# Convolution tables in row halves: Toeplitz blocks of 64 rows and 128 columns for pairs of channels

## The chip, the cores and the metric

The kernel runs on one core of one Trainium2 chip. The metric is the device time of one execution in microseconds. The core has a TensorE (PE, with a queue of its own for weight loads, PEld), a VectorE (DVE), a ScalarE (ACT), a GpSimd (POOL) and a SyncE (SP) that here only issues transfers; all share 16 DMA engines. The on-chip memory SBUF has 128 partitions; PSUM, where PE writes its products, has eight banks.

## What is computed

`x` is 32 sequences of 64 channels and 1024 positions. Four residual layers are added to it one after the other; only the first is touched here:

```python
def _L0_cond_ref(u, log_dt, C, log_A_real, A_imag, D, length):
    K = _get_kernel(log_dt, C, log_A_real, A_imag, Lq)   # one filter of 1024 taps a channel
    n = 2 * Lq
    kf = jnp.fft.rfft(K, n=n)
    uf = jnp.fft.rfft(u, n=n)
    y = jnp.fft.irfft(uf * kf[None], n=n)[..., :Lq]
    y = y + u * D[:, None]
    mask = (jnp.arange(Lq)[None, :] < length[:, None]).astype(u.dtype)
    return y * mask[:, None, :]
...
x = x + _L0_cond_ref(x, ...)                  # causal convolution, a filter for each channel
x = x + _L1_cond_ref(x, itok_B_0_15, w1)      # a 1024 x 1024 weight for each sequence, picked by id
x = x + _L2_cond_ref(x, itok_B_1_14, w2)      # the same with other weights
x = x + _L3_cond_ref(x, ...)                  # gated feed-forward with low-rank additions by id
```

So the first layer is, for each of 64 channels, a causal convolution of 32 sequences with a filter of 1024 taps, and the two after it read one 4 MB weight for each sequence. All data are 4-byte floats.

## The kernel before, in words

**The convolution as products.** For one channel the convolution is a lower triangular Toeplitz matrix (1024 x 1024) times a 1024 x 32 matrix of inputs. It is cut into 8 x 8 blocks of 128 x 128. All blocks on one diagonal are equal, so eight blocks are enough. The filter (with 128 zeros ahead of it) lies as one row of `kp` in DRAM; a transfer whose source steps by one element per partition and by one element along the row reads it as a table `hk` of 128 partitions x 1024, in which partition p holds the filter shifted by p. Columns d x 128 to (d+1) x 128 of that table are the block of diagonal d. The inputs `uf` are laid out on the host (`xf`, L1481) with positions inside a block reversed, so that the shift runs the right way.

**`convolve` (L1372)** handles four channels (HA = 4) and is called 16 times; these calls are called groups here, 0 to 15. It loads `uf` for its four channels (512 KB, two buffers), then, for each of two pairs of channels, a tile `hk` (L1385) that holds two tables, 1024 KB, with three buffers (in group 0 each table is a transfer of its own). For each channel eight matmuls (L1404) with a full 128 x 128 block and N = 256, 224, ... 32 moving columns add up in PSUM: diagonal d multiplies the first 8 - d input blocks. Both channels of a pair write one PSUM bank. After each pair DVE multiplies the bank by the length mask into `tmp` (through the helper `tt`, L1172). After both pairs POOL adds the first quarter of the sequences to `x0`, copies the others to `co`, and stores them to `cd` in DRAM.

**Filters.** `kernels(g)` (L1315) makes the filters of 4 or 8 channels (`GROUPS`), nine times in all: POOL and DVE prepare angles and exponents, ACT takes exponentials and sines, PE multiplies (`pk`, L1346 and L1355), ACT copies the product to `ks` (L1364) and stores it to `kp` (L1366). Kernels 0 and 1 are made ahead; `convolve` calls the others through `between` (`more`), ahead of the matmuls of its second pair. ACT also computes the exponentials of the sizes for later kernels (L1249), in an order set by a scheduler.

**First weights.** While the convolution runs, SP also loads weights for the first adapter pass. `first_weights` (L178) yields one 512 KB load at each step, for "own" tiles (16 early ones, four in a tile of `x` that is not yet used, and 7 late ones that exist once the filters are made and `places` is called) and nine tiles of a rotating pool. `fetch(n)` issues n of them: 8 in group 0, two in each of the next three groups, one in each group after that, and two in each of the last two groups (one with each pair); whatever is left is issued after the convolution.

**The first adapter pass** (`adapter`, L297, its matmuls L304) takes 128 weight tiles for two layers in order, 16 column-tiled matmuls each; the tiles that are not yet on chip rotate through the pool as PE frees them. Everything after that (the other three quarters of the sequences, the feed-forward) follows it.

**Order.** PE's program order is the one written in the code (`manual_schedule`); the other engines' orders are the scheduler's. SP issues its transfers in its program's order: where one has to wait for a free buffer or for a store to `kp`, the later ones wait with it.

Of the kernel before, what the change touches and what calls it, by code (L numbers as in the profile page):

```python
# [9 lines left out]
F32 = mybir.dt.float32  # L10
# [9 lines left out]
P = 128  # L20
B, H, L = 32, 64, 1024
NS = 64
KT = L // P
# [8 lines left out]
MB = 4  # L32
MG = 2
NG = FM // MG
EARLY = 16
LEFT_AT = 11
LATE = 7
FIRST_LOADS = 8
MORE_LOADS = 3
ROTATING = 9  # L40
HA = 4
SEG = 2
# [10 lines left out]
KROW = P + L  # L53
# [23 lines left out]
def kernel(  # L77
# [55 lines left out]
    epool = first.enter_context(tc.tile_pool(name="epool", bufs=1, side="right"))  # L133
    early = [epool.tile([P, L], F32, tag=f"e{i}", name=f"early{i}") for i in range(EARLY)]
    early += [
# [995 lines left out]
def convolution(tc, cst, consts, xt, xf, ssm, lens, x0, cd, ps_tile, fetch, places):  # L1131
# [10 lines left out]
    nc = tc.nc  # L1142
    with ExitStack() as ctx:
# [5 lines left out]
        s3 = ctx.enter_context(tc.tile_pool(name="s3", bufs=3))  # L1149
# [14 lines left out]
        def small():  # L1164
            n_small[0] += 1
            return s1.tile([P, H], F32, tag=f"sm{n_small[0]}", name=f"sm{n_small[0]}")
# [4 lines left out]
        def tt(o, a, b, op):  # L1171
            nc.vector.tensor_tensor(o, a, b, op)  # L1172
            return o
# [80 lines left out]
        x, y = small(), small()  # L1254
# [6 lines left out]
        t, em, ep = small(), small(), small()  # L1261
# [110 lines left out]
        def convolve(kp, row, ha, between):  # L1372


            uf = s3.tile([P, HA, KT, B], F32, tag="uf", name=f"uf{ha}", bufs=2)
            nc.sync.dma_start(uf, xf[:, ha : ha + HA])
            if ha == 0:
                fetch(FIRST_LOADS)
            tmp = g0_2.tile([P, HA, KT * B], F32, tag="tmp", name=f"tmp{ha}")
            for i in range(0, HA, 2):  # L1380
                hk = s3.tile([P, 2, L], F32, tag="hk", name=f"hk{ha + i}")

                for j in range(0, 2, 1 if ha == 0 else 2):
                    n = 1 if ha == 0 else 2
                    nc.sync.dma_start(  # L1385
                        hk[:, j : j + n],
                        bass.AP(
                            tensor=kps.tensor,
                            offset=kp[row + i + j : row + i + j + 1, 1:2].offset,
                            ap=[[1, P], [KROW, n], [1, L]],  # L1390
                        ),
                    )

                first, last = ha <= HA * MORE_LOADS, ha > H - HA * MORE_LOADS
                if ha and i == 0:
                    fetch(1 + first)
                elif ha and last:
                    fetch(1)
                if i:
                    between()  # L1400
                ps = ps_tile(f"pc{ha + i}").rearrange("p (i t) -> p i t", i=2)
                for j in range(2):
                    for d in range(KT):
                        nc.tensor.matmul(  # L1404
                            ps[:, j, d * B :],
                            hk[:, j, d * P : (d + 1) * P],
                            uf[:, i + j, : KT - d, :].rearrange("p k b -> p (k b)"),
                            start=(d == 0),
                            stop=(d == KT - 1),
                        )  # L1410
                tt(
                    tmp[:, i : i + 2, :],
                    ps,
                    maskf.unsqueeze(1).to_broadcast([P, 2, KT * B]),
                    ALU.mult,
                )
            xv = x0.rearrange("p k (b h) -> p k b h", h=H)[:, :, :, ha : ha + HA]
            tv = tmp.rearrange("p i (k b) -> p k b i", b=B)[:, :, :BC, :]
            nc.gpsimd.tensor_tensor(xv, xv, tv, ALU.add)
            co = g0.tile([P, NCK - 1, HA * KT, BC], F32, tag="co", name=f"co{ha}")  # L1420
            tv = tmp.rearrange("p i (k c b) -> p c (i k) b", k=KT, b=BC)[:, 1:]
            nc.gpsimd.tensor_copy(co, tv)
            nc.gpsimd.dma_start(
                cd.rearrange("c p g e -> p c g e")[:, :, ha // HA],
                co.rearrange("p c i b -> p c (i b)"),
            )
# [14 lines left out]
        maskf = mask.rearrange("p k b -> p (k b)")  # L1441
        for g, n in enumerate(GROUPS):
            h0 = sum(GROUPS[:g])

            def more():
                if len(ready) < min(g + 3, len(GROUPS)):
                    ready.append(kernels(len(ready)))
                    if len(ready) == len(GROUPS):
                        making.close()
                        places()  # L1450

            for i in range(0, n, HA):
                convolve(ready[g], i, h0 + i, more)
# [20 lines left out]
def _layouts(np, v):  # L1474
    cont = np.ascontiguousarray

    x = v["x"]

    xt = x.reshape(NCK, TC, KT, P).transpose(3, 0, 2, 1)

    xf = x.reshape(B, H, KT, P)[..., ::-1].transpose(3, 1, 2, 0)  # L1481

    def states(a):
        return np.concatenate([a.T, a.T])
# [58 lines left out]
    for i, (m0, m1) in enumerate(BLOCKS):  # L1543
        n = 2 * (m1 - m0)
        ad[:, i, :, :n] = a[:, :, :, m0:m1].reshape(NE, P, n, R)
    left = left.reshape(P + REST, NE, R).transpose(1, 0, 2)
    n = 2 * BLOCKS[0][1]
# [71 lines left out]
```

## Time and profile before

| what | us |
|---|---|
| median of 3 runs | 2312.29 (2309.24 to 2312.61) |
| the profiled execution's span | 2313.8 |
| PE busy in it | 2249.8 |
| first and last convolution matmul (`pc`, start) | 29.1 and 193.8 |
| convolution matmuls, busy | 153.3 |
| first adapter pass | 195.8 to 329.8 |
| granted TensorE clock, mean | 0.998 |

PE and PEld are the TensorE's matmuls and weight loads; each 4-byte matmul instruction appears as two records in the trace. `pc` is the PSUM tile of the convolution, `pa` that of an adapter, `pk` that of the filters. "L1404" is line 1404 of the kernel. A line of a time view gives busy microseconds and, in brackets, the number of records; a wait is put down to what released it.

### The profile page before, as it was taken

The numbers are of one execution on the slowest core, as the hardware profiler recorded it, in microseconds if no ns is written. First come the engines' busy times: TensorE is split into PE (matmuls) and PEld (weight loads), VectorE is DVE, ScalarE is ACT, GpSimd is POOL, SyncE is SP. The second block draws the span as 40 slices with busy tenths as digits, with TensorE's granted clock in tenths as the row PEclk, the third lists the DMA queues.
The fourth block names the chain that finished last, engine by engine and source line by source line (L and its number), as shares of the span: only waits on it lengthen the run. The fifth ranks groups of instructions, "written<-read, shape, count | busy, mean of one in ns | idle before, by whom it ended". The sixth has DMA issues, their size and how long they took to land.

```text
span 2313.8 us, 53743 instructions
## 1 busy us (share of the span) xinstructions
PE 2249.8 (97%) x21706; PEld 1868.0 (81%) x21706; DVE 1320.6 (57%) x2791; ACT 380.0 (16%) x822; POOL 270.6 (12%) x388
## 2 busy tenths in 40 slices
PE   5999989999999999999999999999999999999999
PEld 4996557787777789688778889688769889799998
DVE  7511127567446776546535676646535676477585
ACT  4300001011001112111102212121102212121220
POOL 3423003111101121000000011000000011100000
PEclk9999999999999999999999999999999999999999
DMA  8999997879997957879997957879997947285582
GB/s 306 354 370 394 407 403 280 317 289 354 365 343 293 350 174 258 304 285 360 350 357 279 358 167 265 297 292 358 355 351 288 363 152 276 87 298 203 191 280 68
DMA packets 201802, 684.96 MB, mean 296 GB/s; under 512 B 26178, under 2 KB 28482, under 8 KB 201042
## 3 DMA queue, kind: packets, MB, share of 16 engines
q1 hardware_dynamic: 169714, 590.77, 69.5%
q0 software_dynamic: 25184, 82.37, 9.6%
q10 hardware_dynamic: 6656, 8.39, 1.0%
q8 instruction: 171, 2.80, 0.5%
q14 instruction: 77, 0.63, 0.1%
HBM read 614.02 MB, written 67.40 MB: 295 GB/s over the span
## 4 chain that ended last, share of the span: by engine, by line
PE 78%; DMA 14%; issue 5%; DVE 2%; POOL 1%; POOLq 0%; SPq 0%; ACT 0%; DVEq 0%
PE pq L664 28%; PE po L1063 22%; PE pa L304 11%; DMA wa<-in_w 7%; PE pc L1404 5%; PE pf L573 5%; PE pr L797 3%; DMA wa<-sums 2%; DMA sums<-kept 1%; PE pe L456 1%; DMA hk<-kp 1%; PE pl_d L427 1%; DMA kp<-ks 1%; DMA wf<-in_wg 0%; DMA wr<-in_wr 0%
## 5 line engine op out<-in xcount | busy, mean ns | idle before, releaser
L304 PE MATMUL pa<-wa,x 128*32 128x256 f32 x7760 | 449.1, 381 | 19.3 <-DMA wa<-in_w 16.8
L664 PE MATMUL pq<-xd,wa 128*128 128x128 f32 x3360 | 415.9, 275 | 1.3 <-DMA wa<-sums 0.9
L304 PEld LDWEIGHTS pa<-wa,x 128*32 128x32 f32 x7760 | 241.8, 110 | 209.9 <-DMA wa<-in_w 49.1
L664 PEld LDWEIGHTS pq<-xd,wa 128*128 128x128 f32 x3360 | 395.0, 192 | 2.3 <-DMA wa<-sums 2.2
L664 PE MATMUL pq<-xd,wb 128*128 128x128 f32 x2520 | 324.1, 276 | 0.6 <-DVE x L316 0.4
L664 PEld LDWEIGHTS pq<-xd,wb 128*128 128x128 f32 x2520 | 300.7, 192 | 4.7 <-DVE x L316 0.6
L314 DVE STREAM_TRANSPOSE y<-pa 128x512 f32<-128x512 f32 x64 | 45.9, 717 | 286.6 <-PE pa L304 286.6
L1063 PE MATMUL po<-act,wd 128*128 128x256 f32 x640 | 168.6, 386 | 0.0
L1404 PE MATMUL pc<-uf,hk 128*128 128x256 f32 (+7 forms) x1024 | 153.3, 312 | 12.2 <-DMA hk<-kp 9.5
L1063 PE MATMUL po<-actd,s 128*128 128x256 f32 x640 | 164.2, 379 | 0.0
L1063 PE MATMUL po<-actd,wd 128*128 128x256 f32 x640 | 164.2, 379 | 0.0
L1404 PEld LDWEIGHTS pc<-uf,hk 128*128 128x128 f32 x1024 | 148.4, 195 | 16.6 <-issue 7.9
L355 POOL DMA_INDIRECT bgu<-in_bgu,rows x44 | 51.4, 1168 | 924.0 <-PE pe L456 827.2
L573 PE MATMUL pf<-xd,wf 128*128 128x256 f32 x640 | 150.9, 381 | 0.0
L1063 PEld LDWEIGHTS po<-act,wd 128*128 128x128 f32 x640 | 117.8, 190 | 29.9 <-issue 14.6
L482 DVE TENSOR_TENSOR s<-wd 128x256 f32<-128x256 f32 x80 | 33.8, 423 | 184.1 <-PE po L1063 184.0
L573 PEld LDWEIGHTS pf<-xd,wf 128*128 128x128 f32 x640 | 121.2, 191 | 17.4
L1063 PEld LDWEIGHTS po<-actd,s 128*128 128x128 f32 x640 | 121.6, 190 | 16.5
L1063 PEld LDWEIGHTS po<-actd,wd 128*128 128x128 f32 x640 | 121.6, 190 | 16.5
L1095 ACT COPY uo<-po 128x256 f32<-128x256 f32 x48 | 17.9, 373 | 622.3 <-PE po L1063 620.2
L573 PE MATMUL pf<-xd,s 128*128 128x256 f32 x480 | 115.9, 385 | 3.9 <-DVE up L607 2.7
L573 PEld LDWEIGHTS pf<-xd,s 128*128 128x128 f32 x480 | 91.0, 191 | 20.0 <-DVE up L607 4.4
(235 smaller groups left out, 2566.4 us busy)
## 6 DMA issues: line engine op xcount, KB each, us to landing
wa<-in_w SPq DMA_DIRECT2D x485, 512.0 KB, 7.0
wa<-sums SPq DMA_DIRECT2D x210, 512.0 KB, 5.8
wb<-parts SPq DMA_DIRECT2D x120, 384.0 KB, 5.3
wd<-in_wd SPq DMA_DIRECT2D x80, 512.0 KB, 7.0
wb<-in_wq SPq DMA_DIRECT2D x90, 384.0 KB, 5.9
hk<-kp SPq DMA_DIRECT2D x30, 1024.0 KB, 8.8
sums<-kept POOLq DMA_DIRECT2D x30, 1024.0 KB, 7.2
wf<-in_wg SPq DMA_DIRECT2D x20, 512.0 KB, 7.1
```

Of the source, the lines that this page charges most:

```text
L304: nc.tensor.matmul(acc[i * S : (i + 1) * S, s * 256 : (s + 1) * 256], xs[c][:, kt, lo + s * S : lo + (s + 1) * S], wt[:, i * 256 : (i + 1) ...
L314: nc.vector.transpose(y, acc)
L355: nc.gpsimd.indirect_dma_start(out=t, out_offset=None, in_=table, in_offset=bass.IndirectOffsetOnAxis(ap=at_, axis=0),)
L427: nc.tensor.matmul(ps[pair(j)], at[:, i, pair(j)], x_i[:, 2 * H * j : 2 * H * (j + 1)], start=(i == 0), stop=(i == n - 1),)
L456: nc.tensor.matmul(ps[:, at_ * 2 * H : (at_ + 1) * 2 * H], bt[pair(j), g], tms[table][pair(j)], start=(g == 0), stop=True, skip_group_chec ...
L482: nc.vector.tensor_add(s1, a21, a22)
L573: nc.tensor.matmul(ps, ws[j][:, kt, :], xb[j][:, kt, :], start=start and kt == 0, stop=kt == KH - 1, skip_group_check=True,)
L664: nc.tensor.matmul(ps[:, to * TQ : (to + 1) * TQ], w[i][:, k, :], xb[:, j, SLOT[i], k, :], start=start and k == 0 and to == 0, stop=k == K ...
L797: nc.tensor.matmul(ps, wts[i][:, kt, :], xs[c][:, kt, :], start=(kt == 0), stop=(kt == KT - 1),)
L1063: nc.tensor.matmul(pss[j], *term, start=(s0 == m0 and i == 0 and home[j] % 2 == 0), stop=(end and i == len(terms) - 1 and not late), skip_ ...
L1095: nc.scalar.copy(u1, p1)
L1404: nc.tensor.matmul(ps[:, j, d * B :], hk[:, j, d * P : (d + 1) * P], uf[:, i + j, : KT - d, :].rearrange("p k b -> p (k b)"), start=(d == ...
```

## The change

One row block of the Toeplitz matrix is now 64 rows high and 128 columns wide. A pair of channels shares one table tile: channel 0 of the pair lies on partitions 0 to 63, channel 1 on partitions 64 to 127, each with 64 + 1024 columns. Each half is loaded by a transfer of its own (64 x 1088, 278.5 KB), and there are four buffers of the tile. Inputs are laid out the same way: partitions 0 to 63 hold channel 0 of the pair, 64 to 127 channel 1, and positions are split into 64-row blocks of even and odd number; the bytes of `uf` are the same. A pair takes 16 steps of 64 rows, and each step is two matmuls, one on each row half, that write to two different PSUM banks. A bank now holds one channel of each of the group's two pairs, so both evictions come after the second pair.

There are two more early tiles (18), and `fetch` is called otherwise: 8 in group 0 and two in every group after it, until none is left.

```diff
-EARLY = 16
+EARLY = 18
 LEFT_AT = 11
 LATE = 7
 FIRST_LOADS = 8
-MORE_LOADS = 3
+PAIR = 2
+HP = P // PAIR
...
-            uf = s3.tile([P, HA, KT, B], F32, tag="uf", name=f"uf{ha}", bufs=2)
-            nc.sync.dma_start(uf, xf[:, ha : ha + HA])
+            uf = s3.tile([P, HA // PAIR, 2, KT * B], F32, tag="uf", name=f"uf{ha}", bufs=2)
+            nc.sync.dma_start(uf, xf[:, ha // PAIR : (ha + HA) // PAIR])
             if ha == 0:
                 fetch(FIRST_LOADS)
             tmp = g0_2.tile([P, HA, KT * B], F32, tag="tmp", name=f"tmp{ha}")
-            for i in range(0, HA, 2):
-                hk = s3.tile([P, 2, L], F32, tag="hk", name=f"hk{ha + i}")
-
-                for j in range(0, 2, 1 if ha == 0 else 2):
-                    n = 1 if ha == 0 else 2
+            halves = [slice(r * HP, (r + 1) * HP) for r in range(PAIR)]
+            banks = [ps_tile(f"pc{ha}_{r}").rearrange("p (i t) -> p i t", i=HA // PAIR) for r in range(PAIR)]
+            for i in range(HA // PAIR):
+                hk = s3.tile([P, HP + L], F32, tag="hk", name=f"hk{ha}_{i}", bufs=4)
+                for r in range(PAIR):
+                    h = row + PAIR * i + r
                     nc.sync.dma_start(
-                        hk[:, j : j + n],
+                        hk[halves[r]],
                         bass.AP(
                             tensor=kps.tensor,
-                            offset=kp[row + i + j : row + i + j + 1, 1:2].offset,
-                            ap=[[1, P], [KROW, n], [1, L]],
+                            offset=kp[h : h + 1, 1:2].offset,
+                            ap=[[1, HP], [1, HP + L]],
                         ),
                     )
-
-                first, last = ha <= HA * MORE_LOADS, ha > H - HA * MORE_LOADS
                 if ha and i == 0:
-                    fetch(1 + first)
-                elif ha and last:
-                    fetch(1)
+                    fetch(2)
                 if i:
                     between()
-                ps = ps_tile(f"pc{ha + i}").rearrange("p (i t) -> p i t", i=2)
-                for j in range(2):
-                    for d in range(KT):
+                for e in range(-1, PAIR * KT - 1):
+                    k0 = (e + 1) // 2
+                    for r in range(PAIR):
                         nc.tensor.matmul(
-                            ps[:, j, d * B :],
-                            hk[:, j, d * P : (d + 1) * P],
-                            uf[:, i + j, : KT - d, :].rearrange("p k b -> p (k b)"),
-                            start=(d == 0),
-                            stop=(d == KT - 1),
+                            banks[r][:, i, k0 * B :],
+                            hk[halves[r], (e + 1) * HP : (e + 1) * HP + P],
+                            uf[halves[r], i, e % 2, : (KT - k0) * B],
+                            start=(e < 0),
+                            stop=(e == PAIR * KT - 2),
+                            skip_group_check=True,
                         )
+            for r in range(PAIR):
                 tt(
-                    tmp[:, i : i + 2, :],
-                    ps,
-                    maskf.unsqueeze(1).to_broadcast([P, 2, KT * B]),
+                    tmp.rearrange("p (i r) t -> p r i t", r=PAIR)[:, r],
+                    banks[r],
+                    maskf.unsqueeze(1).to_broadcast([P, HA // PAIR, KT * B]),
                     ALU.mult,
                 )
...
-    xf = x.reshape(B, H, KT, P)[..., ::-1].transpose(3, 1, 2, 0)
+    xf = x.reshape(B, H // PAIR, PAIR, KT, 2, HP)[..., ::-1]
+    xf = xf.transpose(2, 5, 1, 4, 3, 0).reshape(P, H // PAIR, 2, KT * B)
```

## The prediction

> **What bounds the kernel now.** I read the time slices first, then the chain that ended last, then busy time by stage, the waits and the transfers. The slices say that the PE is saturated nearly everywhere except at the start; in the first four slices (0 to 231 us) the DMA engines are as busy as the PE.
>
> ```profile
> PE   5999989999999999999999999999999999999999
> ...
> DMA  8999997879997957879997957879997947285582
> ```
>
> The last work to end is PE work in the feed-forward part, which this change does not touch; the convolution is 5% of that chain through its matmuls and 1% through its tables. So the change can only move the moment at which everything after the convolution starts, and what is left to load then. Cut out of the chain, the convolution (times are start and length in us) reads:
>
> ```profile
> 37.07 7.53 DMA kp<-ks
> ...
> 46.21 11.11 DMA hk<-kp
> ...
> 61.17 9.05 DMA hk<-kp
> ...
> 82.04 18.52 PE pc L1404 x128
> ...
> 101.22 18.52 PE pc L1404 x128
> ```
>
> 128 matmul records are two groups of four channels, so a group costs the PE 9.26 us and a pair of channels 4.63; where the chain shows `hk<-kp`, the PE waits for a table. Counted from the end in records, the runs at 82.04 and 101.22 hold groups 5 to 8: group 7 ends at 101.22 + 9.26 = 110.5. Group 1 starts at 41.2 (pairs 1 and 2 run as one from 36.57 for 9.38 us). Groups 1 to 7 thus took 69.3 us for 64.8 of matmuls; groups 8 to 15 took 83.6 (the last matmul ends at 194.1) for 74.1.
>
> Busy time by stage (window; length; PE, PEld, DVE, ACT, POOL; clock, DMA share, GB/s):
>
> ```profile
> 60.00:90.00 30.00, 26.45 (x184) 25.66 (x184) 21.21 (x38) 18.30 (x26) 14.69 (x17) 0.94 0.95 337
> 90.00:120.00 30.00, 30.00 (x232) 29.28 (x231) 7.18 (x13) 1.44 (x4) 9.68 (x12) 1.00 0.98 374
> ...
> 150.00:195.00 45.00, 41.49 (x291) 39.77 (x289) 6.23 (x9) 0.00 (x0) 9.74 (x13) 1.00 1.00 391
> ...
> 195.00:330.00 135.00, 123.52 (x2058) 68.14 (x2059) 22.08 (x37) 4.08 (x4) 16.68 (x29) 1.00 1.02 401
> ```
>
> PE and DMA are both full here. A group moves 2.10 MB of tables, 0.52 of `uf`, about 0.52 of one first weight and 0.39 of `cd`: 3.54 MB in 9.26 us, 382 GB/s, which is the measured rate. The last row is the first adapter pass: it runs at the DMA's pace.
>
> **The change part by part.**
>
> *Matmuls.* 16 steps of two 64-row halves replace 2 x 8 full-array instructions; the records double to 2048, and the lengths N are the same list twice per step. If the two halves run side by side, a pair still costs 4.63 us. The nearest row is the row-tiled gather product: 32 records of 128 columns, four row tiles to four banks, in 1.39 us.
>
> ```profile
> 337.36 1.39 PE L456 MATMUL pe<-tm_g,bgu 32*128 32x128 f32 x32
> ```
>
> One every 36 ns or so, where the pc records come every 144.7 ns (18.52/128): row tiles do overlap. I cost this at 0; if they did not, it costs 148 us (a rival below).
>
> *Bytes.* 34 table loads of 33.6 MB in all become 64 loads of 64 x 1088 x 4 = 278.5 KB, 17.8 MB. A group now needs 1.114 MB of tables, 0.92 MB of `uf` and `cd`, and its first weights at 0.524 MB.
>
> *Rate.* Here the change can turn on itself: every table load lands on 64 partitions, and no load of the stage before does. The nearest rows are 64-partition loads later in the kernel:
>
> ```profile
> 1335.50:1337.50 2.00, 2.00 (x16) 1.92 (x16) 1.58 (x7) 0.27 (x1) 0.83 (x1) 1.00 0.90 209
> 1337.50:1344.00 6.50, 6.50 (x69) 5.58 (x71) 6.28 (x13) 1.04 (x1) 0.00 (x0) 1.00 1.03 255
> 1345.00:1347.00 2.00, 2.00 (x11) 1.77 (x10) 1.93 (x7) 0.29 (x1) 0.00 (x0) 1.00 1.01 397
> ```
>
> The first is one 64-partition load from SP: 209 GB/s with the engines 90% busy. The second mixes two such loads by gather (0.51 MB) with 1.13 MB on 128 partitions; at the third row's 397 GB/s those take 2.85 us and leave 3.65 us for 0.51 MB, 140 GB/s. [...] I take the row, 209; the ends are 140 and the full 385.
>
> *Groups 1 to 7.* The order of SP's instructions after the change issues 23 first weights among these (31 in all before `uf` of group 7, less 8 at the start), where before it was about one each. Full-width `uf` + `cd`: 0.917 MB at 385 GB/s = 2.4 us a group. A weight: 1.36 us. Tables at 209: 5.33 us. DMA time: 7 x (2.4 + 5.33) + 23 x 1.36 = 85.4 us, against the 69.3 these groups took: **+16.1**. At 140 the tables take 7.96 and the sum is 103.8, +34.5; at 385, 2.9 and 68.4, -0.9. Group 0 has the same DMA time as before (8 weights; 2.23 MB at 209 is 10.7 us, 4.2 MB at 385 is 10.9), so group 1 starts as before.
>
> *Table stores.* The changed order on ACT puts kernel 2's copy and store behind the exponential of kernel 4's sizes, and kernel 3's behind that of kernel 6. Before, these exponentials ran at 43.23 and 64.72 and the stores were issued at 37.07 and 52.80. So the stores move to at most about 44 and 62, and kernel 2's lands some 6 us later. SP waits for it in order, with `uf`, later tables and weights behind:
>
> ```profile
> SPq L1385 <- DMA kp<-ks: 11.6, 2, 8.7
> ```
>
> SP idle is DMA idle in a stage that now lacks DMA time. Bounds 0 (the queue is deep enough) and +8 (all 6 us and part of the second); I take **+4**; at the full rate 2.
>
> *Groups 8 to 15.* Only 7 weights fall here. DMA: 8 x 7.73 + 7 x 1.36 = 71.4 us; PE: 74.1 + 1.3 for the last two kernels' matmuls (0.66 each) = 75.4, against 83.6. At most -8.2; with 4 us of slack some of the table waits stay, so **-5** (at 140: 92.4 us of DMA, +9; at full rate -7).
>
> *First adapter pass.* Two more first weights, and the eight late ones that still landed until about 200, 6 us after the last pc, have landed before. Before: 6.1 us of pending loads + 92 tiles x 1.31 us (0.524 MB at 401 GB/s) = 126.6 from the convolution's end. After: 90 tiles = 117.9, and SP has nothing to load until the first rotating tile comes free, about 0.7 + 2.9 us after the end: 121.5. **-5.** With the PE as cover: it was busy 123.5 of these 135 us, so no more than this comes off.
>
> *Evictions.* As many of the same size (0.70 us), but both at a group's end: at the convolution's end two stand before POOL's add, **+0.7**. Inside, PE needs a bank again only several groups later. SP's 30 extra table issues at about 0.5 us are 15 us in 165, in which SP waits for PE anyhow: 0.
>
> *Sum.* 16.1 + 4 - 5 - 5 + 0.7 = +10.8 on the profiled 2313.8 us (its span, which the runs' 2312.29 median lies 1.5 below): 2324.6, so **2323** as a median.
>
> **The rivals.** A measurement of this kernel tells about 0.2% (4.6 us) from no change.
>
> 1. *Half-width loads at the full rate, or near it; faster.* A mix with full-width loads could fill what half-width ones leave idle. Then -0.9 + 2 - 7 - 5 + 0.7 = -10: 2302. For it: half the table bytes, and the middle window's 255 GB/s for a mix. Against it: 209 with little else in flight. It decides above about 330 GB/s (groups 1 to 7: 71 us).
> 2. *Balance.* At 285 GB/s the tables take 3.91 us a group, groups 1 to 7 need 75.5 us (+6.2), and 6.2 + 3.5 - 5.5 - 5 + 0.7 is nil: 2312. It holds between 245 and 330.
> 3. *Mixed loads at the gathers' 140 GB/s; much slower.* 34.5 + 9 + 4 - 5 + 0.7 = +43: 2355. For it: this is the only window with half and full widths mixed. Against it: gathers by POOL are another kind of transfer.
> 4. *The row halves don't run at once.* 32 pairs x 4.63 = +148, less the DMA terms that it would hide: about 2445. The row-tiled product speaks against it.
>
> **How the numbers follow.** Tables at 160 to 245 GB/s, my forecast: 0.50, own range 2317 to 2340. Gather-like, below 160: 0.17. Balance: 0.14. Faster: 0.16. Serial halves: 0.03. So slower 0.70, same 0.14, faster 0.16. The range runs from rival 1's value to just past rival 3's, 2302 to 2356; it leaves out about half of each, and rival 4.
>
> **What would show it.** In the changed profile: pc at about 18.5 us per 256 records where nothing waits; between 41 and 111 us the DMA share near 1 but GB/s well under 385 (23 weights, 7.8 MB of tables, 6.4 of the rest: 26 MB in 85 us, near 310); PE waits on `hk<-kp` there, not late; group 7 ending near 130; kernel 2's store at 43 to 44. The first pa would start at 195.8 + 16 = 212 and the pass take about 5 us less. The forecast is wrong if that stage moves more than 340 GB/s, if the first pa starts before 200, or if table loads take no longer per byte than weights.

## The result

The changed kernel takes 2341.8 us (four runs, 2336.7 to 2349.2) where the kernel before takes 2312.0: the ratio is 1.0137, with a 95% interval of 1.0112 to 1.0162, so it is slower by about 30 us. The forecast was 2323 in a range of 2302 to 2356, with 7 chances in 10 for slower. Direction and range held; the size was a third of what was measured.

The time slices of the profile after, over 2335.1 us (that execution took 2336.7):

```profile
span 2335.1 us, 55827 instructions
...
PE   5699989999999999999999999999999999999999
...
DMA  7987998889997965879998966889997957376582
```

In the second slice (58 to 117 us) PE has fallen from 9 tenths to 6. The DMA engines are at 8 and 7 tenths in the third and fourth slices (117 to 234 us), where they stood at 9: PE and the DMA engines both have idle time in the convolution now, at different moments. Two windows of the same profile say where (window; length; PE, PEld, DVE, ACT, POOL busy; clock, DMA share, GB/s). They are cut at the group borders that the matmul records show, groups 1 to 7 (pairs 2 to 15) and groups 8 to 15 (pairs 16 to 31):

```profile
42.70:141.00 98.30, 76.82 (x972) 75.53 (x972) 37.33 (x75) 26.64 (x40) 29.98 (x37) 0.86 0.93 263
141.00:223.50 82.50, 78.67 (x1068) 77.63 (x1070) 10.39 (x17) 0.72 (x2) 19.16 (x24) 0.96 0.74 221
```

The same groups of the kernel before:

```profile
41.20:115.00 73.80, 69.56 (x523) 67.59 (x522) 43.14 (x74) 28.27 (x41) 32.05 (x37) 0.98 0.94 341
115.00:194.10 79.10, 75.95 (x554) 73.82 (x557) 11.07 (x16) 0.72 (x2) 19.27 (x24) 1.00 1.00 382
```

The forecast ends group 7 of the kernel before at 110.5 us. In the matmul records pair 15, its last, runs from 110.4 to 115.1, so the forecast's two bases, 69.3 and 83.6 us, hold 13 and 17 pairs instead of 14 and 16.

Groups 1 to 7 take 98.3 us instead of 73.8 (+24.5). Groups 8 to 15 take 82.5 instead of 79.1 (+3.4), though the DMA engines are busy for only 0.74 of that time. So transfers crowd in the first half of the stage and are missing in the second. The convolution ends at 223.5 instead of 194.1 (+29.4), and the feed-forward's first work (`pl_g`, right after the adapter pass) starts at 359.6 instead of 331.7 (+27.9). What comes after that was 6.7 us shorter in this execution (1975.4 against 1982.1), but it lies between 1973.5 and 1987.5 in the profiles of the experiments below, so one execution of each kernel doesn't show a gain there.

The matmuls themselves are as fast as before. Where nothing waits, a pair of channels takes 4.77 us from its first record to its last, before and after, though the records have doubled (the kernel before, then the changed one; behind the second bar stands PE's idle time ahead of these matmuls):

```profile
L1404 PE MATMUL pc<-uf,hk 128*128 128x256 f32 (+7 forms) x1024 | 153.3, 312 | 12.2 <-DMA hk<-kp 9.5
L1402 PE MATMUL pc<-uf,hk 64*128 64x64 f32 (+7 forms) x2048 | 165.0, 320 | 29.8 <-issue 15.4
```

The 165.0 us of busy time against 153.3 come from first pairs after a wait, which run at a lower granted clock (0.63 to 0.74 on average over the five pairs of the table below). Pair 6, for one, starts at 69.59 us after a wait of 6.0, and the clock around its start is half of the full one:

```profile
66.10:72.90 6.80, 3.31 (x16) 3.34 (x18) 5.75 (x12) 4.54 (x9) 0.54 (x2) 0.50 0.57 162
```

Of the idle time, 29.8 us against 12.2, the very first pair has 4.4 (before: 4.8). Nearly all the rest falls on five pairs:

| pair (group) | PE idle before it, us | the pair itself, us |
|---|---|---|
| 6 (3) | 6.0 | 6.5 |
| 8 (4) | 6.0 | 6.5 |
| 10 (5) | 3.4 | 7.4 |
| 12 (6) | 5.7 | 7.1 |
| 24 (12) | 3.8 | 7.6 |
| any other from 13 to 23 | 0 to 0.6 | 4.8 |

In SP's order four or five first weights stand behind the inputs and tables of each of the groups 2 to 5, and so ahead of those of groups 3 to 6. Four of the seven late ones stand ahead of the inputs of group 12.

What SP waited for most between 40 and 142 us (line, what ended the wait, us in total, times, longest):

```profile
SPq L1387 <- DMA kp<-ks: 22.2, 2, 12.3
SPq L1387 <- DMA early<-in_w: 11.2, 8, 2.1
```

The first is the wait for the late stores to `kp` that the forecast names. The second is a table load that waits for the landing of a first weight, with which it shares no data: in this trace the transfers of SP and the stores of ACT share eight completion semaphores, and none of the 66 between 40 and 142 us starts before the transfer ahead of it on its semaphore has landed. The table load at 82.27 us, for one, has the semaphore of the first weight issued at 74.56, eight places ahead of it, which landed at 82.26.

### The profile page after: what moved, and what is told of

It reads as the page before. It is cut to its first block, busy times and chain, and to the rows that moved or that the text cites. A ratio compares the mean times of both kernels' runs of the same rounds, so it can differ in the third digit from the quotient of the medians.

```text
span 2335.1 us, 55827 instructions
## 1 busy us (share of the span) xinstructions
PE 2256.5 (97%) x22730; PEld 1881.4 (81%) x22730; DVE 1314.7 (56%) x2791; ACT 379.6 (16%) x822; POOL 269.8 (12%) x388
## 4 chain that ended last, share of the span: by engine, by line
PE 79%; DMA 8%; issue 2%; DVE 1%; POOL 0%; POOLq 0%; SPq 0%; DVEq 0%
PE pq L665 28%; PE po L1064 23%; PE pa L305 13%; PE pf L574 8%; DMA wa<-in_w 7%; PE pr L798 3%; PE pe L457 2%; PE pl_d L428 1%; DMA sums<-kept 1%; DMA wr<-in_wr 0%; PE pl_g L428 0%; PE pl_u L428 0%; PE po L1072 0%; PE pe_rest L457 0%; POOLq L390 0%
## 5 line engine op out<-in xcount | busy, mean ns | idle before, releaser
L1402 PE MATMUL pc<-uf,hk 64*128 64x64 f32 (+7 forms) x2048 | 165.0, 320 | 29.8 <-issue 15.4
L1402 PEld LDWEIGHTS pc<-uf,hk 64*128 64x128 f32 x2048 | 161.2, 198 | 32.9 <-issue 19.7
```

The costliest lines, as they stand in the source:

```text
L1402: nc.tensor.matmul(banks[r][:, i, k0 * B :], hk[halves[r], (e + 1) * HP : (e + 1) * HP + P], uf[halves[r], i, e % 2, : (KT - k0) * B], sta ...
```

## The experiments

Three theories were to be told apart. A, the forecast's: table loads on 64 partitions are slow. B: the place of the first weights in SP's queue. C: the late table stores. D, the fall of the clock after each wait, was added on seeing the profile. All ratios are to the kernel before on the same chip.

### e1 and e3: one load over 128 partitions

```diff
-                for r in range(PAIR):
-                    h = row + PAIR * i + r
-                    nc.sync.dma_start(
-                        hk[halves[r]],
-                        bass.AP(
-                            ...
-                            ap=[[1, HP], [1, HP + L]],
+                h = row + PAIR * i
+                load = nc.sync.dma_start(
+                    hk,
+                    bass.AP(
+                        ...
+                        ap=[[KROW, PAIR], [1, HP], [1, HP + L]],
```

In e1 the weights are tied (with an order of issue, not a wait) about where the changed kernel has them; in e3 they are spread evenly as in e2.

> The changed kernel with one edit of substance: both halves of a table tile come by one load over all 128 partitions (32 loads instead of 64, the same bytes), and the first weights stand in nearly the same places of SP's order (23 of them among groups 1 to 5 or 7). Theory A, the forecast's: table loads on 64 partitions at about 209 GB/s are what makes groups 1 to 7 wait. Then table bytes now move at about 385 GB/s, the DMA time of these groups falls by 7 x 2.4 = 17 us, and the time from 2342 to about 2324 (2318 to 2328). Theory B, the place of the weights in the queue: tables stand behind four or five weights a group whatever their own rate, the stalls of five pairs stay, and the time stays at 2335 to 2342.

> Both edits at once: one 128-partition load for a table tile, and two weights a group. DMA time of a group 2.4 + 2.9 + 2.7 = 8.0 us, below PE's 9.3. Theories A and B: PE bounds the convolution except where a table store is late; its end at about 188 to 193 instead of 194 before the change, and the adapter pass 2 to 5 us shorter; time 2300 to 2309, faster than before the change. Theory C: the stalls around the stores of the third and fourth filters stay at 10 us or more, time 2315 or more.

Measured: 2587.4 us (1.1185, 1.1161 to 1.1209) and 2588.5 us (1.1190, 1.1166 to 1.1215). No theory had expected a loss of 275 us, and as a test of the width both failed. A stretch of e1 in which little but table loads is under way (the second line is the rate in 40 slices of 440 to 453 us):

```profile
DMA  9985211111111111011110111111111111111111
GB/s 356 367 216 153 78 27 54 54 54 54 54 54 54 54 54 54 40 54 54 54 54 40 54 54 54 54 53 52 52 52 53 54 54 54 54 54 54 54 52 52
```

The load moves 54 GB/s at a tenth of the 16 engines' time, as if two of them did the work: 2/16 of the 401 GB/s that the adapter pass moved is 50, as an estimate, and 54 were measured. The source pattern of this load begins with the pair, 2; that of the kernel before, whose window in e6 moved 390 GB/s, begins with the 128 partitions. Whether this is the reason was not tried. So the half bytes at full rate, the premise of the forecast's first rival, stayed untested.

### e2: two weights a group

```diff
-                if ha and i == 0:
-                    fetch(2)
+                if ha:
+                    with tc.issue_after(load.ins):
+                        fetch(1)
```

(`load` is the second half's table load of each pair.) The changed kernel asks for two weights a group too, but nothing ties them to it: the scheduler puts 3, 5, 4, 5, 5, 1, 0, 0, 0, 0, 4, 3, 0, 0 between the `uf` loads of groups 1 to 15. With the tie it is 3 and then 2 throughout.

> The changed kernel with its 64-partition loads, but the first weights are tied behind the table loads of their own group, one behind each pair's, so that two a group are issued through all groups instead of three to five in groups 1 to 6, none in 7 to 10 and seven in 11 and 12. Theory A: the DMA time of a group is 2.4 + 5.3 + 2 x 1.36 = 10.4 us against 9.3 to 9.6 of PE, so the convolution ends at about 43 + 15 x 10.4 = 199 instead of 223, time about 2318 (2312 to 2324). Theory B: with no crowd ahead of the tables PE is the bound but for the waits for table stores; convolution's end about 193 to 196, time 2305 to 2311. Theory C, the late table stores on ACT alone: 2335 to 2342.

Measured: 2330.2 us, 1.0067 (1.0044 to 1.0089). The order alone gives back 12 of the 30 us, with the stores as late as in the changed kernel (43.60 and 62.20 us); theory C is out as the whole cause, B in its pure form missed by 19 or more, and A, with 2324 as its upper end, by 6. The convolution ends at 214.6. From 82 to 200 us:

```profile
82.00:200.00 118.00, 108.00 (x1408) 106.52 (x1406) 19.55 (x31) 4.78 (x9) 28.19 (x34) 0.94 1.03 278
```

Now the DMA engines are full all through this window, and PE still waits 2 to 3 us in every second group or so. Groups 8 to 15 take 95.1 us with the wait ahead of them, 11.9 each, where the sum of rates gave 10.4. With 3.08 MB a group that is 259 GB/s: two weights a group are more than a stage with half-width tables can carry at PE's pace, and even the even order leaves 17 us of the loss.

### e4: the stores early

```diff
-            with behind(*((stored, 1 if g > 1 else -1) if g < 4 else (turned, g - 1))):
+            with behind(*((stored, 1 if g > 1 else -1) if g < 4 else (turned, g - 1))), behind(stored, g // 2 if g in (4, 6) else -1):
                 done = nc.scalar.activation(rho, rho, AF.Exp)
```

> The changed kernel with one edit: ACT takes the third and fourth filters' copies and stores ahead of the exponentials behind which they had come to stand, as before the change. Theory C: SP's waits for stores (35 us in the changed kernel, 12.3 at the longest, with the DMA engines idle for some 10 of them) fall, and with them the time by 8 to 12 us, to about 2332. The forecast's own term was 4 us: about 2338. Theories A and B allow less than 5.

Measured: 2343.3 us (2332.1 to 2348.7), 1.0122 (1.0082 to 1.0163): no change against the changed kernel's 1.0137. The edit did less than it was meant to. The stores of kernels 2 and 3 went out at 41.47 and 60.07 us instead of 43.74 and 62.35, not at the 37.07 and 52.80 of the kernel before, because ACT still takes the next kernel's sines ahead of them. SP's waits for stores over the first 330 us of e4:

```profile
SPq L1387 <- DMA kp<-ks: 27.5, 3, 10.4
SPq L171 <- DMA kp<-ks: 12.1, 2, 7.8
```

They sum to 39.6 us; in the changed kernel they were 35.2 (30.9 and 4.3). So 2.3 us less delay is worth nothing that e4's runs, 17 us apart, can show, and on the whole delay e4 doesn't decide; e9 and e10 do, below.

### e5 and e6: the kernel before, with half-width loads, and the control

```diff
-                for j in range(0, 2, 1 if ha == 0 else 2):
-                    n = 1 if ha == 0 else 2
+                for j in range(2):
+                    lo = j * (P // 2)
                     nc.sync.dma_start(
-                        hk[:, j : j + n],
+                        hk[lo : lo + P // 2],
                         bass.AP(
                             tensor=kps.tensor,
-                            offset=kp[row + i + j : row + i + j + 1, 1:2].offset,
-                            ap=[[1, P], [KROW, n], [1, L]],
+                            offset=kp[row + i : row + i + 1, 1 + lo : 2 + lo].offset,
+                            ap=[[1, P // 2], [KROW, 2], [1, L]],
```

e6 keeps the original lines with `range(2)` and `n = 1` in all groups: as many loads of as many bytes, over 128 partitions.

> The kernel before, whose table tiles of 128 partitions and 1024 KB now come by two loads of 64 partitions and 512 KB each; all else, the order on SP too, as before. Theory A (a load on 64 partitions moves at about 205 GB/s): a group's DMA time goes from 9.2 to 2.10 MB/205 + 1.44 MB/385 = 13.9 us, 15 groups take 66 us longer less the first ones' slack, time about 2375 (2360 to 2395). If only the number of loads mattered, it would be as e6.

> The control: the kernel before, whose table tiles come by two loads of 128 partitions and 512 KB each, one for each channel (as it has them in its first group already). The number of loads and the bytes of each are those of e5. Theory A: nothing but SP's 30 more issues, time 2310 to 2316. If the number of loads is what costs (more waits for a free slot among the loads under way), 2330 or more.

Measured: e5 2387.2 us, 1.0316 (1.0296 to 1.0337), +74 us. e6 2316.1 us, 1.0010 (1.0002 to 1.0019), 2.8 us more, at the edge of what was expected. The same window of both, e5 first:

```profile
110.00:190.00 80.00, 64.97 (x428) 62.26 (x428) 8.31 (x13) 1.09 (x3) 11.91 (x15) 0.90 1.03 258
```

```profile
110.00:190.00 80.00, 79.55 (x580) 77.61 (x579) 11.38 (x17) 0.72 (x2) 21.50 (x27) 1.00 1.01 390
```

Both keep the DMA engines busy all the time, for 258 and for 390 GB/s. From the start of pair 15 to that of pair 27 of e5 are 86.6 us, 14.4 a group; less 3.7 us for the 1.44 MB at full width, 10.7 us remain for 2.10 MB: 196 GB/s, if the full-width loads beside them keep their 385. That is near the forecast's 209, and the loss is the width's, not the number of loads'. (In e5's trace the stores of kernels 2 and 3 went out late too, at 43.70 and 61.47 us; pairs 15 to 27 lie behind that.)

### e7: filler for the clock

```diff
+                if i == 0 and ha // HA in FILL:
+                    for _ in range(5):
+                        nc.tensor.matmul(banks[0][:, 0, :246], cst[:, :P], cst[:, :246], start=True, stop=True, skip_group_check=True)
                 for e in range(-1, PAIR * KT - 1):
```

> e2 (two weights a group) with five 128 x 128 matmuls of 246 columns on a constant ahead of groups 2, 4, 8, 10, 12 and 13, in which e2's PE waits 1.9 to 2.9 us for a table and then takes 6.3 to 6.7 us for the first pair instead of 4.8; 2 us of filler each, whose results are overwritten. Theory D (the fall of the clock after a wait is a cost of its own): the six first pairs take 4.8 again, 6 x 1.7 = 10 us less, about 2320. Theory A (the DMA engines bound these groups, so a faster PE only waits longer): no change, 2327 to 2333, with the pairs at 4.8 and longer waits ahead of later pairs.

Measured: 2330.1 us, 1.0073 (1.0057 to 1.0090), the same as e2's 2330.2; the convolution ends at 214.8 (e2: 214.6). The granted clock of the run rose from 0.996 to 0.998, and the filled first pairs took 4.8 to 4.9 us again, but other pairs waited instead (pair 6 for 2.9 us, pair 18 for 2.0, where e2 had 0.1 and none), and the convolution did not end earlier. The slow first pairs were a symptom: with the DMA engines setting the pace, the faster PE waited longer.

### e8: the two halves on two queues

```diff
-                    load = nc.sync.dma_start(
+                    load = (nc.scalar if r and ha >= 16 else nc.sync).dma_start(
                         hk[halves[r]],
```

> e2 with the second half of each table tile loaded by ACT's queue instead of SP's from group 4 on, so that loads of the lower and the upper 64 partitions are under way at once. [...]

Measured: 2334.0 us, 1.0096 (1.0064 to 1.0129), not better than e2. From 100 to 200 us, e8 and then e2:

```profile
100.00:200.00 100.00, 90.90 (x1224) 89.69 (x1223) 13.23 (x22) 1.08 (x3) 22.70 (x28) 0.97 1.03 275
```

```profile
100.00:200.00 100.00, 90.00 (x1149) 88.92 (x1148) 12.42 (x20) 1.09 (x3) 22.22 (x27) 0.93 1.03 273
```

275 against 273 GB/s, where full-width loads moved 390 in e6: from two queues at once the halves gained nothing that shows.

### e9 and e10: each part of the change alone

e9 has the change's tables, loads and matmuls, 16 early tiles and the weights about where the kernel before has them. e10 has the kernel before with its weights where the changed kernel has them, two fewer among groups 1 to 7, as it has two early tiles fewer. Both tie them to the table loads of a group:

```diff
+PACE = {...}   # e9: 2 in groups 1 to 3, 1 in 4 to 13, 2 in 14, the last ones in 15
+               # e10: 3, 5, 4, 5, 4 in groups 1 to 5, 4 in 11, 3 in 12
...
+                if ha:
+                    with tc.issue_after(load.ins):
+                        fetch(PACE...)
```

> The change's tables, loads and matmuls alone: 16 early tiles again and the first weights where the kernel before has them in SP's order (8, then 2 or 3 a group at first, one a group after that, nine in the last group). By the forecast's terms a group takes 2.4 + 1.114 MB/209 + 1.36 = 9.1 us of DMA, as before (half the bytes at half the rate), so no loss is left: 2310 to 2316. If a mix of half-width and full-width loads moves at the 260 GB/s that e2 showed, it takes 2.56 MB/260 = 9.8 us, 0.5 us above PE's pace over 15 groups: 2317 to 2322. If the half width costs more still than that: above 2324.

> The other part alone: the kernel before, its tables, loads and matmuls, with its first weights moved to where the changed kernel has them in SP's order (21 in groups 1 to 5, none in 6 to 10, seven in 11 and 12). Full-width tables take 2.10 MB/385 = 5.45 us a group, just what the forecast gave the half-width ones, so the crowd should cost as much: groups 1 to 7 take 7 x (2.4 + 5.45) + 21 x 1.36 = 83.5 us of DMA against 69.3: 2320 to 2330. If the crowd hurts only with half-width loads: 2310 to 2316.

Measured: e9 2314.8 us, 1.0008 (0.9990 to 1.0027). e10 2338.2 us, 1.0101 (1.0080 to 1.0122). This is the main result. The new layout alone, with its slow half-width loads, costs nothing that can be measured (by the interval at most 0.27%, 6 us). The weights' order alone, with full-width loads and no other change, costs 24 of the 30 us, more than the 2320 to 2330 that were expected. The other 6 us appear only with both together. Groups 1 to 7 and groups 8 to 15 of e10:

```profile
42.35:131.33 88.98, 72.90 (x523) 70.07 (x522) 44.48 (x77) 27.10 (x39) 31.67 (x37) 0.92 0.94 348
131.33:218.00 86.67, 77.72 (x554) 75.39 (x557) 11.06 (x16) 0.72 (x2) 19.07 (x24) 0.96 0.84 297
```

The same of e9:

```profile
42.66:119.50 76.84, 70.90 (x972) 69.64 (x971) 40.11 (x75) 26.36 (x39) 28.33 (x35) 0.96 0.93 247
119.50:195.93 76.43, 75.72 (x1064) 74.32 (x1068) 9.90 (x17) 0.72 (x2) 19.68 (x24) 1.00 1.00 290
```

e10 shows the pattern of the changed kernel: DMA busy and PE waiting first, DMA idle afterwards, the end of the convolution at 218.0. In its groups 1 to 7 the DMA engines were busy for 0.94 of 89.0 us, 83.6 us, as the expected sum of 83.5 had it; what that sum left out are 5.3 us of idle DMA engines there and 7.6 us more in groups 8 to 15. In e9 groups 1 to 7 take 3.0 us longer than in the kernel before and groups 8 to 15, at PE's pace, 2.7 us less. Its adapter pass takes 3.5 us longer, for a reason that was not looked for, and the feed-forward starts 5.4 us later in this execution; what follows was 6.3 us shorter, within the spread named above.

e2 and e9 have the same tables and nearly as many weights, 38 and 36. Up to 178 us e2 has issued 35 of them and e9 27; e9 issues its last nine behind the last table of the convolution, as the kernel before does with eight. e2 takes 17 us more than the kernel before, e9 none. So an even spread is not the best place either.

The two also decide on theory C. In the trace e10 issues the stores of kernels 2 and 3 at 38.23 and 52.76 us, as the kernel before does, and loses 24 us; e9 issues them at 43.41 and 62.00, nearly as late as the changed kernel, and loses nothing in all.

### e11 and e12: the stores on another queue

```diff
-            done = nc.scalar.dma_start(
+            done = nc.gpsimd.dma_start(
                 kp[:, P:].rearrange("h (a b) -> a h b", b=LQ), ks[:, :n]
```

> e2 (the changed kernel with two weights a group) with the filters' stores issued by POOL instead of ACT, so that they take no slot among the eight that the loads of SP and the stores of ACT share. In e2 SP waited 40 us in all for stores. If these waits are what keeps e2 above the kernel before, 5 to 12 us come off: 2318 to 2325. If the DMA engines are full anyhow: 2327 to 2333.

> The kernel before with the same edit, as a candidate that could beat both: SP waited 28 us for stores in it, PE 8 us for tables in the convolution. If the waits for slots cause the stalls at pairs 5 and 7, 3 to 5 us come off: 2307 to 2310. If the convolution's end hangs on the DMA engines' 370 to 390 GB/s alone: 2311 to 2314.

Measured: e11 2341.9 us, 1.0115 (1.0094 to 1.0136), 11 us worse than e2 by the ratios. e12 2316.6 us, 1.0006 (0.9993 to 1.0020), no difference. Neither expectation of e11 held: SP still waited 38.5 us for stores (e2: 39.7), and kernel 2's was issued at 46.6, later than on ACT. Whether that is all of the 11 us was not tried. No version here beats the kernel before.

## Why the prediction was right or wrong

**Right: slower, by the DMA engines, in groups 1 to 7.** 24.5 of the 29.4 us by which the convolution ends later arise there. The step that names 23 first weights among these groups as what overfills the queue is what e10 shows alone.

**Right: the matmuls at nothing.** 4.77 us a pair before and after. The serial-halves rival is out.

**Right: the rate of a half-width load.** 196 GB/s in e5 for the 209 taken. The rivals that hang on the rate being 330 or more, 245 to 330, or 140, are out for this transfer.

**Luck: the range.** The forecast's own case had 2317 to 2340 and just missed 2341.8. The range holds because its upper end stands for tables at 140 GB/s, which e5 rules out.

**Wrong in emphasis: "here the change can turn on itself".** The forecast's own sums said otherwise. Half the bytes at half the rate are the same DMA time: 1.114 MB at 209 is 5.33 us, 2.10 MB at 385 is 5.45. The width cancels what the halving saves, and e9 shows just that. What is left over is the number of weights per group and where they stand. The forecast had both in one sum and gave the blame to the rate.

**Misread: the border between groups 7 and 8.** The runs of matmuls at 82.04 and 101.22 begin with the second pair of a group, behind a kernel's `pk` matmuls; the forecast took them to begin with the first. That made its base for groups 1 to 7 short by 4.5 us and the other one long by 4.5. Its +16.1 is +11.6 on the right base, its -5 is -0.5, and at most -3.7 could come off groups 8 to 15, not -8.2. The two errors cancel in its sum.

**Mis-sized: groups 1 to 7, 85.4 us of DMA time and 4 for the stores.** That is +15.6 on the right base; measured +24.5. The window has 98.3 us at a DMA share of 0.93, which is 91.4 us busy and 6.9 idle. So 2.9 us of the miss are idle DMA engines and 6.0 are transfers that took longer than their own rates add up to. (From 41 to 111 us, where the forecast looked for near 310 GB/s, 265 moved at a DMA share of 0.90.) The same shows between 90 and 120 us, with the DMA engines never idle:

```profile
90.00:120.00 30.00, 20.95 (x262) 20.64 (x261) 3.15 (x7) 3.08 (x5) 4.01 (x5) 0.84 1.03 299
```

These 30 us moved 9.0 MB, of which 2.05 MB were tables by the size of their packets; at 209 and 385 GB/s that is 9.8 + 18.0 = 27.8 us (28.5 with e5's 196). Where half-width and full-width loads mix, the sum of their rates was about 5 to 8% too short. The packets of 4096 bytes on SP's queue, which are full-width here, took 209 ns on average in this window, against 170 in the same window of the kernel before. Why a mix is slower, and how that depends on how the two alternate, stays open.

**The stores: as forecast, but not the cause of the loss.** They moved to 43.74 and 62.35 us and SP waited for them. e9, with the same delay and no crowd, is 3.0 us late in groups 1 to 7: its PE waits 4.1 us ahead of pair 6 and loses 2.1 to that pair's slow start, where the kernel before waits 3.6 ahead of pair 7 and loses 1.6. What the delay costs alone was not tried, so the +4 is neither shown nor refuted.

**Mis-sized, and of the wrong sign: groups 8 to 15.** Measured +3.4. The forecast took the seven weights there as spread over eight groups; they come in a burst at 170 to 180 us, four of them ahead of group 12's inputs and tables, and that group had 3.8 us of waiting and 2.8 of slow start. e9, without the burst, has 76.4 us there, -2.7.

**Mis-sized: the adapter pass, -5.** From the convolution's end to the feed-forward's first work: 137.7 us before, 136.2 after, -1.5. (The forecast's sum for the kernel before, 126.6 us, left some 11 us out of these 137.7; its difference of -5 rests on the two tiles and the start.) The fewer bytes are there (52.2 MB against 55.1), but with all 38 tiles loaded there is nothing to move until PE frees one:

```profile
210.00:225.00 15.00, 14.02 (x198) 13.50 (x194) 2.58 (x4) 0.00 (x0) 2.59 (x4) 1.00 0.15 51
225.00:230.00 5.00, 4.33 (x52) 2.31 (x56) 0.00 (x0) 0.00 (x0) 4.33 (x7) 0.66 0.49 151
```

The DMA engines lie nearly idle for the last 15 us of the stage, and the pass starts at half their rate and a clock of 0.66. The forecast had counted 3.6 us of this and not the slow start.

**Not counted: group 0, +1.5** (it ends at 42.7 instead of 41.2). With the four terms: 24.5 + 1.5 + 3.4 - 1.5 = 27.9, the delay at the feed-forward's first work.

## What to carry to other kernels

Before crediting a layout with fewer bytes, divide them by the rate at which its transfers move: half the bytes on half the partitions took the same time here (5.33 us a group at 209 GB/s, as an estimate, against 5.45 at 385; e9, 1.0008, shows no difference). Where a scheduler fills a queue, a request in the code is not a place in the queue: two loads a group became five a group, and the place of these loads, not the layout, made the kernel slower (two a group, held evenly, still cost 17 us; fewer a group, with nine behind the last table, cost nothing that shows); tying each prefetch to a transfer of its own group is one line. When two parts of a change go together, run each alone on the other's base: that settled here what the sums had mixed up.

## What the runs showed of the hardware that was not expected

- A load whose source pattern has the pair of channels as its slowest dimension ran at 54 GB/s on a tenth of the DMA engines' time, and made the kernel 275 us slower (2587 and 2588 us in e1 and e3; the rate is e1's), at the same bytes and over all 128 partitions.
- Full-width loads were slower beside loads on 64 partitions: the changed kernel moved 299 GB/s where its transfers' own rates give 323 (an estimate, 9.0 MB in 27.8 us), with the DMA engines busy throughout, and 4096-byte packets took 209 ns on average instead of 170.
- After waits of 3.4 to 6.0 us in the changed kernel PE's next pair took 6.5 to 7.6 us instead of 4.8, with the granted clock at 0.50 around the start of pair 6; pair 7 of the kernel before took 6.4 after 3.6 us, and pair 30, after 2.5 us, took 4.8. Filling six such waits with other matmuls changed nothing (e7), because the wait was for transfers.
